# Self-attention over 4 x 4096 positions in float32: the weights' and x's split forms moved in SBUF to other addresses modulo 256 bytes

## The chip, the cores and the metric

One core of one Trainium2 chip. The metric is the device time of one execution in microseconds, as the median of several runs. Profiles are of one further execution, recorded by the hardware profiler.

## The reference

x has the shape (4, 64, 64, 256) in float32: B = 4 images of N = 4096 positions with C = 256 channels; q and k have C2 = 128 channels.

```python
q = jnp.einsum('bwhc,cd->bwhd', x, Wq) + bq
k = jnp.einsum('bwhc,cd->bwhd', x, Wk) + bk
v = jnp.einsum('bwhc,cd->bwhd', x, Wv) + bv
pq = q.reshape(B, -1, N)
pk = k.reshape(B, -1, N)
pv = v.reshape(B, -1, N)
energy = jnp.einsum('bcn,bcm->bnm', pq, pk)
attention = jax.nn.softmax(energy, axis=-1)
out = jnp.einsum('bcm,bnm->bcn', pv, attention)
out = out.reshape(B, W, H, C)
return gamma * out + x
```

## The kernel before

**Three forms of every operand.** Matmuls run on values of the type float32r. To keep float32's precision, each operand is split into three forms, numbered f = 0, 1, 2: h (the value scaled by a little under 1, rounded on writing), l (what is left) and d (a scaled difference of the two). A product of two operands is the sum of three matmuls, one for each f, added up in PSUM. The split is an ACT instruction (h) and two DVE instructions (l and d).

**Projections.** An image is projected in NI = 16 units i of 256 positions. For each unit, `transposed` (L186) makes four TensorE transposes into PSUM, `x_forms` (L193) splits the result into the tile `xf` of shape [128, 3, KC = 2, 2, 128], and `products` (L209) multiplies it with the weights' forms in the tile `wf` (L117). With w = 0 it makes q and k together: `xf` is the stationary operand, a 128x128 block, and the moving operand is `wf` of w = 0, 256 columns. With w = 1 it makes v: a 128x128 block of `wf` of w = 1 is stationary, and `xf` is moving, 256 columns. So each unit has 12 matmuls of 256 columns for each w, 24 in all, each with a weight load of its own, and the whole kernel has 1,536; they all stand at L222. The weights are split once, in `weights` (L159). DVE adds the bias of q and k in `seed_qk` (L233), ACT that of v in `seed_v` (L240), and `qk_forms` and `v_forms` split the results and send them to HBM (image 0 keeps v in SBUF).

**Attention.** The loop at L567 has B x STEPS = 512 steps n, 128 to an image: eight groups of 512 queries, and in each 16 steps over pairs of 128 keys. In a step, TensorE's work stands in this order: `cross` of step n+2 (L298, two matmuls, the part with f = 2 of the energies; ACT scales each at L299), `attend(n, 0)` (six matmuls at L355, accumulators `a` and `b`), `energy` of step n+2 (four matmuls at L313, f = 0 and 1; ACT's exponential at L316), what `step(n, "pe")` gives of the next image's projection, and `attend(n, 1)` (six more at L355). In `cross` and `energy` the stationary operand is the tile `k`, the moving one `q`; in `attend` the stationary operand is `vall` (named `v` in the profile) and the moving one `h` or `ld`, the forms of the exponentials, made by ACT (L322) and DVE (L336, L338). All these 9,216 matmuls have 512 columns. TensorE takes them in this order; a weight load for the next matmul can run while the present one streams.

**Projections between the steps.** Image 0 is projected ahead of the loop (L517 to L565). The units of image b+1 are spread over image b's steps, one unit to R = 8 steps: of the step's number r modulo 8, r = 0 transposes, r = 3 and 5 bring four products (f = 2) and r = 4 and 6 eight (f = 0 and 1). At the end of each group of 16 steps, `sums` (L384) adds up the softmax's denominators with two matmuls that have the constant `ones` as stationary operand and `zf` as moving one.

**Where the tiles lie.** A pool's tiles lie one behind the other in SBUF in the order in which their tags are first used, and the pools one behind the other: the constants, then `qkv` (`v`, `wf`), `ppool` (`x`, `ld`, `s`, `h`; the `xf` of image 0 uses `ld`'s buffers), `work` (`o`, `pf`, `q`, `xin`, `xf` of the other images, `r` with `zf`) and `kpool` (`k`). The constants end at byte 19,200 of each partition, 75 x 256. `ident` and `ones` start 128 bytes past a multiple of 256. Every tile of the later pools has a size that is a multiple of 256 bytes, so all of them start at a multiple of 256, and so does every slice that a matmul of L222, L298, L313 or L355 reads (the slices are steps of 512 or 1,024 bytes).

Of the kernel before, what the change touches and what calls it, by code (L numbers as in the profile page):

```python
# [10 lines left out]
F32R = mybir.dt.float32r  # L11
# [9 lines left out]
def kernel(  # L21
# [37 lines left out]
    B, W, H, C = x.shape  # L59
    P = 128  # L60
# [3 lines left out]
    KC = C // P  # L64
# [36 lines left out]
    with ExitStack() as fast:  # L101
# [4 lines left out]
        qkv = pool("qkv", 1)  # L106
        ppool = pool("ppool", 2)
        work = pool("work", 2)
# [5 lines left out]


        vall = qkv.tile([P, NU, 3, 2, C], F32R, tag="v", name="v")
        wf = qkv.tile([P, 2, 3, KC, C], F32R, tag="wf", name="wf")  # L117
        zd, rd = (dram.tile([B * NG, NB], F32, tag=n, name=n, bufs=1) for n in ("zd", "rd"))
        xs4 = work.tile([P, 4, 2, XB], F32, tag="o", name="xs", bufs=1)
        raw = ppool.tile([P, 2, KC, C], F32, tag="x", name="raw")  # L120
        scaled = ppool.tile([P, 2, KC, C], F32, tag="x", name="scaled")
# [29 lines left out]
        def split(h, l, d, y, scale=E):  # L151

            nc.scalar.activation(h, y, AF.Identity, scale=UPPER * scale)
            yield
            for t, f in ((d, 1.0 / scale + 1.0), (l, 1.0 / scale)):
                nc.vector.scalar_tensor_tensor(t, h.bitcast(F32), -f, y, ALU.mult, ALU.add)  # L156
                yield

        def weights(w):  # L159

            nc.scalar.mul(scaled[:, w], raw[:, w], E ** -(w + 1))
            yield from split(*(wf[:, w, f] for f in range(3)), scaled[:, w])

        def image(b):
            for g in range(NG):
# [5 lines left out]
        def bank(name, shape):  # L171
            pool, tag = next(now["banks"])
            return pool.tile(shape, F32, tag=tag, name=name)
# [19 lines left out]
        def x_forms(b, i):  # L193

            y = units.pop(("xt", b, i))
            if b == 0:
                f = ppool.tile([P, 3, KC, 2, P], F32R, tag="ld", name=f"xf_{b}_{i}")
            else:
                f = work.tile([P, 3, KC, 2, P], F32R, tag="xf", name=f"xf_{b}_{i}", bufs=1)
            units["xf", b, i] = f  # L200
            h = f[:, 0]
            nc.scalar.activation(h, y, AF.Identity, scale=UPPER)  # L202
            yield
            nc.vector.scalar_tensor_tensor(f[:, 2], h.bitcast(F32), 1.0 + E, y, ALU.mult, ALU.subtract)
            yield
            nc.vector.tensor_tensor(f[:, 1], y, h.bitcast(F32), ALU.subtract)
            yield

        def products(b, i, w, fs):  # L209

            xf = units["xf", b, i]
            if fs[0] == 2:
                units[w, b, i] = bank(f"qv{w}_{b}_{i}", [P, 2, C])
            to = units[w, b, i]
            for f in fs:
                for s in range(2):
                    for k in range(KC):
                        if w:
                            left, right = wf[:, 1, f, k, s * P : (s + 1) * P], xf[:, f, k]
                        else:  # L220
                            left, right = xf[:, f, k, s, :], wf[:, 0, f, k]
                        nc.tensor.matmul(  # L222
                            to[:, s, :],
                            left,
                            right.rearrange("p s a -> p (s a)") if w else right,
                            start=(f == 2 and s == k == 0),
                            stop=(f == 1 and k == KC - 1),
                            skip_group_check=True,
                        )
# [237 lines left out]
        def step(n, engine):  # L467
# [5 lines left out]
            if engine == "pe" and b < B:  # L473
                if r == 0:
                    transposed(b, i)
                elif r == 3:
                    products(b, i, 0, (2,))
                elif r == 4:
                    products(b, i, 0, (0, 1))
                elif r == 5:  # L480
                    products(b, i, 1, (2,))
                elif r == 6:
                    products(b, i, 1, (0, 1))
            elif engine == "act" and b < B:
                if r == 1:
                    made["x"] = x_forms(b, i)
                    next(made["x"])
                    load_x(b, i + 1)
                elif r == 5:
                    made["qk"] = qk_forms(b, i)  # L490
                    next(made["qk"])
                elif r == 6:
                    seed_v(b, i)
                elif r == 7:
                    made["v"] = v_forms(b, i)
                    next(made["v"])
            elif engine == "dve":
                if r == 0 and "v" in made:
                    for _ in made.pop("v"):
                        pass  # L500
                if b < B:
                    if r in (1, 2):
                        next(made["x"])
                    elif r == 3:
                        seed_qk(b, i)
                    elif r == 5:
                        next(made["qk"])
                    elif r == 6:
                        for _ in made.pop("qk"):
                            pass  # L510
                    elif r == 7:
                        next(made["v"])
# [6 lines left out]
        for i in range(3):  # L519
            load_x(0, i)  # L520
        transposed(0, 0)
        first = [weights(0), x_forms(0, 0), weights(1)]
        for pieces in first + [first[0], first[1], first[2]]:
            next(pieces)
        for pieces in first:
            next(pieces)
        for i in range(NI):
            load_x(0, i + 3)
            if i + 1 < NI:
                transposed(0, i + 1)  # L530
                xs = x_forms(0, i + 1)
            else:
                xs = iter(())
# [33 lines left out]
        for n in range(B * STEPS):  # L567
            b, u = divmod(n, STEPS)
# [42 lines left out]
    with tc.If(nc.values_load(again[0:1, 0:1]) > 0), ExitStack() as general:  # L611
# [3 lines left out]
        xpool, xtpool, qkv = pool("gx", 2), pool("gxt", 2), pool("gqkv", 1)  # L615
        ppool, work = pool("gp", NP + 2), pool("gw", 1)
# [86 lines left out]
        for b in range(B):  # L703
# [16 lines left out]
            for g in range(NG):  # L720
                ps = []
                mx = work.tile([P, 2, NB], F32, tag="mx", name=f"gmx_{b}_{g}")
                for t in range(NP):
# [9 lines left out]
                    p = ppool.tile([P, 2, NB], F32, tag="p", name=f"gp_{b}_{g}_{t}")  # L733
# [89 lines left out]
```

## Time and profile before

| | us |
|---|---|
| median of three runs | 2421.97 (2421.10 to 2422.91) |
| the profiled execution, its own time | 2424.35 |
| its span, first to last instruction | 2422.6 |

| lines | engine and operation | count | busy us | mean ns of one |
|---|---|---|---|---|
| L355 | PE matmul, 128x512, three groups | 6,144 | 640.0 + 633.4 + 631.7 | 390 to 394 |
| L313 | PE matmul, 128x512 | 2,048 | 552.0 | 391 |
| L298 | PE matmul, 128x512 | 1,024 | 316.3 | 390 |
| L222, w = 1 | PE matmul, 128x256 | 768 | 117.6 | 290 |
| L222, w = 0 | PE matmul, 128x256 | 768 | 113.9 | 285 |
| L222 | PE weight load, 128x128, both w | 1,536 | 109.1 + 108.8 | 194, 193 |
| L355 | PE weight load, 128x128, three groups | 6,144 | 385.1 + 383.9 + 369.3 | 188, 188, 189 |

Matmuls overlap in the pipeline, so the mean length of one (390 ns) is not the time between two: what counts for the whole is the distance from the start of one to the start of the next, called the pitch below. The granted TensorE clock has a mean of 0.994 of full speed over the span; it is at half speed for three short stretches in the first 114 us and for two at the end. The projection of image 0 fills the first 100 us, in which TensorE is busy for 66.89 us; between us 500 and 1000 it is busy for 495.48.

### The profile page before, as it was taken

To read this page: it belongs to the slowest core of one execution; us is meant where nothing else is said; L and a number is where in the kernel's file an instruction comes from. 1 tells how busy PE (TensorE), PEld (TensorE's weight loads), DVE (VectorE), ACT (ScalarE), POOL (GpSimd) and SP (SyncE) were. 2 spreads that over 40 slices of the span, in tenths; PEclk is the share of its full clock that TensorE was granted. 3 is DMA by queue.
4 is the path that set the end of the run, shared out by engine and by line. 5 is a ranking of instruction groups with operands and counts; after the bars stand their busy time and mean duration, and the time that the engine had idled before them with its cause. 6 is when DMAs were issued, how large, how long until landed. Compare 5 with 4: busy or idle time off the path is not lost.

```text
span 2422.6 us, 31905 instructions
## 1 busy us (share of the span) xinstructions
PE 2358.6 (97%) x11094; PEld 1954.4 (81%) x11094; DVE 2138.0 (88%) x2126; ACT 1870.8 (77%) x3076; POOL 581.7 (24%) x943
## 2 busy tenths in 40 slices
PE   6799999999999999999999999999999999999998
PEld 6688888888888888888888888888888888888886
DVE  7789988889989899888899898898888888888887
ACT  4577777877877877778778778778777778787875
POOL 5422222222322222212233122222123111111110
PEclk9999999999999999999999999999999999999999
DMA  9756655656796666566699566675569644444443
GB/s 200 169 143 166 180 143 158 177 156 181 217 296 171 168 164 181 146 158 178 157 284 265 147 165 166 170 181 147 154 176 315 198 127 131 120 119 125 120 123 92
DMA packets 243990, 413.82 MB, mean 171 GB/s; under 512 B 26031, under 2 KB 141487, under 8 KB 243822
## 3 DMA queue, kind: packets, MB, share of 16 engines
q0 software_dynamic: 203152, 368.77, 57.2%
q1 hardware_dynamic: 40126, 42.67, 6.4%
q8 instruction: 91, 1.49, 0.3%
q14 instruction: 77, 0.63, 0.1%
q10 hardware_dynamic: 544, 0.26, 0.0%
HBM read 306.64 MB, written 104.98 MB: 170 GB/s over the span
## 4 chain that ended last, share of the span: by engine, by line
PE 86%; ACT 9%; DMA 2%; DVE 1%; issue 1%; POOL 0%; SPq 0%; DVEq 0%; ACTq 0%
PE a L355 35%; PE b L355 17%; PE e L313 17%; PE e L298 9%; PE qv L222 7%; ACT o L369 3%; ACT e L299 2%; ACT x L316 1%; ACT h L322 1%; PE z L384 1%; PE xt L191 1%; DMA k<-kf 1%; DMA qd<-f 1%; ACT zf L378 1%; DVE v L156 0%
## 5 line engine op out<-in xcount | busy, mean ns | idle before, releaser
L316 ACT ACTIVATE x<-e 128x512 f32<-128x512 f32 x960 | 523.8, 600 | 319.1 <-PE e L313 316.0
L285 POOL DMA_DIRECT2D k<-kf x512 | 275.8, 539 | 1743.3 <-PE e L313 1638.6
L331 DVE TENSOR_TENSOR s<-s,x 128x1024 f32<-128x1024 f32 x480 | 585.8, 1220 | 95.1 <-ACT x L316 92.7
L299 ACT ACTIVATE e<-e 128x512 f32<-128x512 f32 x1024 | 547.4, 574 | 137.2 <-PE e L298 136.5
L355 PE MATMUL a<-h,v 128*128 128x512 f32 x2048 | 640.0, 394 | 0.0
L355 PE MATMUL a<-ld,v 128*128 128x512 f32 x2048 | 633.4, 390 | 0.0
L355 PE MATMUL b<-ld,v 128*128 128x512 f32 x2048 | 631.7, 390 | 0.0
L336 DVE TENSOR_TENSOR ld<-x,h 128x1024 fp32r<-128x1024 f32 x480 | 585.4, 1220 | 30.9 <-PE b L355 24.8
L338 DVE SCALAR_TENSOR_TENSOR ld<-h,x 128x1024 fp32r<-128x1024 f32 x480 | 584.4, 1218 | 0.0
L313 PE MATMUL e<-q,k 128*128 128x512 f32 x2048 | 552.0, 391 | 4.5
L322 ACT ACTIVATE h<-x 128x1024 fp32r<-128x1024 f32 x480 | 509.9, 1062 | 13.3
L313 PEld LDWEIGHTS e<-q,k 128*128 128x128 f32 x2048 | 379.4, 188 | 98.1 <-ACT e L299 23.2
L355 PEld LDWEIGHTS a<-ld,v 128*128 128x128 f32 x2048 | 385.1, 188 | 83.2
L355 PEld LDWEIGHTS b<-ld,v 128*128 128x128 f32 x2048 | 383.9, 188 | 82.8 <-ACT s L385 1.4
L355 PEld LDWEIGHTS a<-h,v 128*128 128x128 f32 x2048 | 369.3, 189 | 62.7 <-issue 1.0
L298 PE MATMUL e<-q,k 128*128 128x512 f32 x1024 | 316.3, 390 | 0.6 <-DMA k<-kf 0.6
L298 PEld LDWEIGHTS e<-q,k 128*128 128x128 f32 x1024 | 192.0, 188 | 42.3 <-issue 1.6
L222 PE MATMUL qv<-wf,xf 128*128 128x256 f32 x768 | 117.6, 290 | 26.0 <-DVE qv L233 25.9
L222 PEld LDWEIGHTS qv<-wf,xf 128*128 128x128 f32 x768 | 109.1, 194 | 37.4 <-DVE qv L233 29.5
L222 PEld LDWEIGHTS qv<-xf,wf 128*128 128x128 f32 x768 | 108.8, 193 | 7.5
L222 PE MATMUL qv<-xf,wf 128*128 128x256 f32 x768 | 113.9, 285 | 0.0
L270 POOL DMA_DIRECT2D kf<-f x128 | 98.4, 769 | 41.0 <-ACT xf L202 20.6
(79 smaller groups left out, 1215.1 us busy)
## 6 DMA issues: line engine op xcount, KB each, us to landing
k<-kf POOLq DMA_DIRECT2D x512, 384.0 KB, 3.5
vf<-vf POOLq DMA_DIRECT2D x48, 768.0 KB, 6.0
v<-vf POOLq DMA_DIRECT2D x48, 768.0 KB, 7.2
kf<-f POOLq DMA_DIRECT2D x128, 192.0 KB, 3.4
qd<-f POOLq DMA_DIRECT2D x128, 192.0 KB, 3.1
q<-qd POOLq DMA_DIRECT2D x32, 768.0 KB, 4.7
o<-in_x_dram POOLq DMA_DIRECT2D x31, 512.0 KB, 7.7
out_dram<-o SPq DMA_DIRECT2D x31, 512.0 KB
```

Of the source, the lines that this page charges most:

```text
L222: nc.tensor.matmul(to[:, s, :], left, right.rearrange("p s a -> p (s a)") if w else right, start=(f == 2 and s == k == 0), stop=(f == 1 an ...
L270: nc.gpsimd.dma_start(to, f)
L285: nc.gpsimd.dma_start(t, kf[b, u % NU])
L298: nc.tensor.matmul(e, *forms(n, i, 2), start=True, stop=False, skip_group_check=True)
L299: nc.scalar.mul(e, e, -REST)
L313: nc.tensor.matmul(e, *forms(n, i, f), start=False, stop=(f == 1), skip_group_check=True)
L316: nc.scalar.activation(x[:, i, :], e, AF.Exp, scale=(1.0 + E) ** 3 / E)
L322: nc.scalar.activation(h, units[n], AF.Identity, scale=UPPER)
L331: nc.vector.tensor_tensor(s, s, x, ALU.add)
L336: nc.vector.tensor_tensor(l, x, h.bitcast(F32), ALU.subtract)
L338: nc.vector.scalar_tensor_tensor(d, h.bitcast(F32), 1.0 + E, x, ALU.mult, ALU.subtract)
L355: nc.tensor.matmul(to, vall[:, t, f, i, j * P : (j + 1) * P], units[n][f][:, i, :], start=(t == 0 and i == 0 and f != 1), stop=(t == NU - ...
```

## The change

The tile `wf` becomes one flat row of 6 x KC x C + 32 elements (32 elements are 128 bytes). The forms of w = 1 (v) start at its beginning, those of w = 0 (q and k) behind them and 32 elements further. The tile `xf` becomes a flat row of XF = 6C + 16 elements (16 are 64 bytes), of which the forms take the last 6C. The instructions, their order and their shapes stay.

```diff
-        wf = qkv.tile([P, 2, 3, KC, C], F32R, tag="wf", name="wf")
+        wfs = qkv.tile([P, 6 * KC * C + 32], F32R, tag="wf", name="wf")
+        wf = [
+            wfs[:, o : o + 3 * KC * C].rearrange("p (f k c) -> p f k c", f=3, k=KC)
+            for o in (3 * KC * C + 32, 0)
+        ]
...
-            yield from split(*(wf[:, w, f] for f in range(3)), scaled[:, w])
+            yield from split(*(wf[w][:, f] for f in range(3)), scaled[:, w])
+
+        XF = 6 * C + 16
...
             if b == 0:
-                f = ppool.tile([P, 3, KC, 2, P], F32R, tag="ld", name=f"xf_{b}_{i}")
+                f = ppool.tile([P, XF], F32R, tag="ld", name=f"xf_{b}_{i}")
             else:
-                f = work.tile([P, 3, KC, 2, P], F32R, tag="xf", name=f"xf_{b}_{i}", bufs=1)
+                f = work.tile([P, XF], F32R, tag="xf", name=f"xf_{b}_{i}", bufs=1)
+            f = f[:, 16 : 16 + 6 * C].rearrange("p (f k s a) -> p f k s a", f=3, k=KC, s=2)
...
-                            left, right = wf[:, 1, f, k, s * P : (s + 1) * P], xf[:, f, k]
+                            left, right = wf[1][:, f, k, s * P : (s + 1) * P], xf[:, f, k]
                         else:
-                            left, right = xf[:, f, k, s, :], wf[:, 0, f, k]
+                            left, right = xf[:, f, k, s, :], wf[0][:, f, k]
```

## The prediction

> **What bounds the kernel.** I read the page's busy shares first, then the chain that ended last by engine, then that chain in order of time around the lines that the change touches, then the nanosecond start times of the matmuls there.
>
> ```profile
> PE 2358.6 (97%) x11094; PEld 1954.4 (81%) x11094; DVE 2138.0 (88%) x2126; ACT 1870.8 (77%) x3076; POOL 581.7 (24%) x943
> ...
> PE 86%; ACT 9%; DMA 2%; DVE 1%; issue 1%; POOL 0%; SPq 0%; DVEq 0%; ACTq 0%
> ```
>
> TensorE is the bound: 97% busy and 86% of the chain. The time is therefore the number of matmuls times the distance from one start to the next (below: the pitch). No matmul is added or removed, so only the pitch can change. The chain in order of time shows it (start us, length us, what):
>
> ```profile
> 1111.67 0.91 PE a L355 x4
> 1112.58 0.45 PE b L355 x2
> 1113.03 0.91 PE e L313 x4
> 1113.94 0.47 PE qv L222 x4
> 1114.41 0.93 PE a L355 x4
> 1115.34 0.46 PE b L355 x2
> 1115.80 0.45 PE e L298 x2
> 1116.25 0.91 PE a L355 x4
> 1117.16 0.45 PE b L355 x2
> 1117.61 0.91 PE e L313 x4
> 1118.52 0.95 PE qv L222 x8
> ```
>
> Two things are to be seen. Eight 256-wide products of L222 take 0.95, 119 ns each, while four 512-wide matmuls take 0.91, 227 ns each, or 113.5 per 256 columns: the products cost more per column. And right behind products the four `a` matmuls take 0.93 and the two `b` 0.46, against 0.91 and 0.45 elsewhere.
>
> In nanoseconds, as medians over the 48 groups of each kind behind us 100: the undisturbed pitch of a 512-wide matmul is 226.7. A group of four products has 113.4, 119.1, 120.0, 120.0; a group of eight goes on at 120.0. The next five 512-wide matmuls have 233.3, 235.9, 228.4, 232.5, 230.9, and the sixth is back at 226.7. These are the same in all groups to 1 ns, for both kinds of product (w=0 and w=1).
>
> 113.4 is half of 226.7 although each of both runs beside one weight load of the same size, so I take 113.4 per 256 columns as the floor of the moving stream. In the half-clock slices at the start the pitch is 213 and 427, one column per 0.833 ns, without any surplus: what stretches the pitch at full clock is the supply of operands, not the array. What lies above the floor (6.7 per product, up to 9.2 behind them) differs with the moment at which the weight load meets the running stream. The change can act here if that meeting depends on addresses.
>
> **What moves.** From the tile sizes, every tile ahead of and between the pools is a multiple of 256 bytes before, so every operand of L222, L298, L313 and L355 starts at residue 0 modulo 256. Afterwards `wf` is 128 bytes longer, so all that lies behind it moves: `x`, `ld`, `s`, `h`, `q`, `xin` to 128; the `xf` tile is 64 bytes longer and its data lie 64 in, at 192 for image 0 (in an `ld` buffer) and for the others; `r`, `zf` and `k` to 192. `v` and the v form of `wf` stay at 0, the q and k form goes to 128. Stationary minus moving residue then is: products w=1, 0-192 = 64; products w=0, 192-128 = 64; L298 and L313 (`k` against `q`), 64; L355 (`v` against `h` or `ld`), 128. So not 1,536 matmuls change their alignment but all 10,752.
>
> **The cost, part by part.**
> 1. Products behind us 100: 1,152, in 96 groups of four and 96 of eight. Surplus over 113.4 of a group of four 0+5.7+6.6+6.6 = 19 ns, of eight 19+4×6.6 = 45 ns: 96×64 = 6.2 us. If the two streams no longer meet, all of it goes: -6.2 us.
> 2. The five matmuls behind each group: 6.6+9.2+1.7+5.8+4.2 = 27.5 ns, 192 groups: 5.3 us. Four products at 113.4 take exactly two pitches of 226.7 and eight take four, so if step 1 holds the order in which both streams were before is kept, and these go too: -5.3 us.
> 3. Products before us 100: surplus 1.9 us by the same start times. PE waits there for L233 (the table of waits: us in total, times, longest), so a shorter product mostly lengthens that wait; taken as 0, at best -1.9.
>
> ```profile
> PE qv L222 <- DVE qv L233: 25.9, 15, 4.5
> ```
>
> 4. Attention, 9,216 matmuls (L298 1,024, L313 2,048, L355 6,144): undisturbed at the floor now, so there is nothing to win, but each ns lost costs 9.2 us. The nearest row for another residue is L384: `ones` is at 128 and `zf` at 0 (the timeline: start us, length us, instructions, idle time before).
>
> ```profile
> 178.01 0.30 PEld L384 LDWEIGHTS z<-zf,ones 128*128 128x128 f32 x2 [0.89 <-ACT o L369]
> 178.01 0.73 PE L384 MATMUL z<-zf,ones 128*128 128x512 f32 x2 [0.45 <-ACT o L369]
> 178.35 0.59 PEld L191 LDWEIGHTS xt<-ident,x 128*128 128x128 f32 x4
> ```
>
> From the second weight load to the second matmul the 31 pairs have 228 to 236 ns. The first matmul of L313 or L355 behind a pause, at residue 0, has 227 to 240 by the same measure. So 128 apart shows neither better nor worse than 0, at the one moment it can be seen. I take 0 for attention. The bounds: the worst pitch in any row is 235.9, +9.2×9,216 = +85 us; the other way, down to the 213.3 of one column per cycle, -13.3×9,216 = -123 us, which the equal cost per column at 256 and 512 wide speaks against.
> 5. Transfers into moved tiles (`k`, `q`, `xin`, `o`): nothing, since PE waited 0.6 us in all for `k`, which lands in 3.5 us with a step of 4.5 us and three buffers ahead. Without that cover a doubled landing would cost at most 3.5 us per late `k`. DVE and ACT keep their instructions; at 88% and 77% they follow a PE that gains 0.5%.
>
> Sum: -6.2-5.3 = -11.5 us. The profiled execution has 2424.35 us with a span of 2422.6, so 2412.9 and 2411.1; against the median of 2421.97, **2410.5 us**.
>
> The Trainium skill speaks against any effect: "TensorE: Matmul & The Clock Gate", step-by-step list of Part 2, says that TensorE reads moving and stationary operand through two independent SBUF ports and that loading the next weights takes no bandwidth from the running matmul. By that rule the sum would be 0. The surplus of 6.6 ns behind the second product is not explained by it, and no row here shows whether addresses are the cause.
>
> **The rivals.**
> - *The residue changes nothing.* The surplus could come from widths alone: a 256-wide pitch leaves 113 ns for a weight load of about 106 (from the load to the first matmul behind a pause), so each product's stream has a load beside it nearly all the time. For it: w=0 and w=1 have the same pitch though operands swap sides. Against: the first product of each group also carries a full load and sits at the floor. Then products and the five behind them stay: 2422, or 2419 to 2425 with a shifted order. The skill's two ports give the same time.
> - *Attention loses its order (slower).* All operands share one residue now, and every run between disturbances settles to exactly 226.7. After the change, the pair of moving and stationary residue switches from 128 to 64 and back four times per step (from `b` to L298, back to `a`, from `b` to L313, back to `a`). If a switch disturbs the order as a group of products does, its first two matmuls cost 6.6+9.2 = 15.8 ns: 512 steps × 4 × 15.8 = +32 us; less the 11.5 won, **2443 us**. If no stretch of two to six matmuls ever settles, the mean of the five, 5.5 ns, holds for all 9,216: +51 us, 2473. It decides from 1.25 ns per attention matmul (11.5/9,216); from 1.8 ns the kernel is slower by over 0.2%. For it: five to nine matmuls pass after every pause until the pitch is back at 226.7. Against: L384's row above.
> - *Attention gains as well:* 2350 or so, half of the bound in step 4; nothing but the missing row for residue 64 speaks for it.
>
> **Chances.** Forecast (products to the floor, attention as before) 0.45; attention loses its order 0.41; no effect 0.10; attention gains 0.04. What a measurement of this kernel can tell from no change is about 0.2%, 4.8 us. Faster: 0.45 less 0.02 for a partial gain under that bound, plus 0.04 = 0.47; same 0.10+0.02 and less 0.01 for the shifted order = 0.11; slower 0.42. The forecast's own range is 2406 to 2417: from all surplus gone with the 1.9 us of step 3 and some 3 us of the same surplus behind pauses, to half of the gain. The range for 8 in 10 reaches into the slower case, past its 2443, to 2462, which leaves out its upper quarter and the gain on attention: 2405 to 2462.
>
> **What would show it.** Step 1: eight products in the chain at 0.91 instead of 0.95. Step 2: `a` behind products at 0.91, not 0.93. Step 4: four `a` elsewhere still 0.91 and four L313 0.91; if these read 0.93 or more, attention lost its order and the forecast is wrong on the slower side. If everything reads as before, the residue does not matter. PE's waits for `k` above a few us would make step 5 wrong.

## The result and the profile after

| | before | changed |
|---|---|---|
| median, us | 2421.53 (2419.73 to 2422.91, 4 runs) | 2463.19 (2462.48 to 2464.26, 4 runs) |
| span of the profiled execution, us | 2422.6 | 2460.7 |

The changed kernel is slower by the ratio 1.0174, with a 95% interval of 1.0161 to 1.0186. Its line numbers differ, as do those of the kernels further down: L222 has become L229, L298 L305, L313 L320 and L355 L362.

The page's busy shares, its chain by engine and three of its groups, of the changed kernel:

```profile
PE 2399.0 (97%) x11094; PEld 1952.7 (79%) x11094; DVE 2142.7 (87%) x2126; ACT 1875.3 (76%) x3076; POOL 582.7 (24%) x943
...
PE 87%; ACT 9%; DMA 1%; DVE 1%; issue 1%; POOL 0%; SPq 0%; DVEq 0%; ACTq 0%
...
L362 PE MATMUL a<-ld,v 128*128 128x512 f32 x2048 | 647.2, 397 | 0.0
...
L320 PE MATMUL e<-q,k 128*128 128x512 f32 x2048 | 563.8, 397 | 1.5 <-ACT e L306 0.3
...
L362 PEld LDWEIGHTS a<-ld,v 128*128 128x128 f32 x2048 | 386.9, 189 | 89.8
```

TensorE is the bound as before, with the same number of instructions and 40 us more of busy time (2399.0 against 2358.6); DVE and ACT differ by 5 us. The matmuls of `ld` with `v` take 397 ns where they took 390, those of `q` with `k` 397 where they took 391. The weight load beside them has stayed at 188 to 189 ns.

The chain in order of time, the changed kernel around its products:

```profile
1127.79 0.46 PE b L362 x2
1128.25 0.93 PE e L320 x4
1129.18 0.47 PE qv L229 x4
1129.66 0.92 PE a L362 x4
1130.58 0.46 PE b L362 x2
1131.04 0.46 PE e L305 x2
1131.50 0.94 PE a L362 x4
1132.44 0.46 PE b L362 x2
1132.90 0.93 PE e L320 x4
1133.83 0.94 PE qv L229 x8
```

The four `a` of 1131.50, with eight matmuls between them and the last product, take 0.94 where the kernel before had 0.91 in that place, four L320 take 0.93 where L313 had 0.91, two L305 0.46 where L298 had 0.45. The eight products take 0.94 instead of 0.95. So it is not the products, for whose operands the pads were put in, that changed most, but attention's matmuls.

A stretch without any product shows it alone: the last image's steps have none. The windows of both kernels, first before, then changed (us, busy time and number of PE, PEld, DVE, ACT and POOL, granted clock, DMA share, GB/s):

```profile
1900.00:2400.00 500.00, 495.84 (x2170) 404.79 (x2169) 436.70 (x390) 394.25 (x641) 74.75 (x132) 1.00 0.48 126
```

```profile
1900.00:2400.00 500.00, 496.07 (x2115) 395.57 (x2114) 426.82 (x383) 388.77 (x629) 78.62 (x139) 1.00 0.50 131
```

In the same 500 us, at the same granted clock of 1.00, TensorE starts 2,115 matmuls instead of 2,170, though it is as busy.

Nearly all of the time can be booked from the start times of the matmuls. The sums of the pitches behind us 100 (a matmul in front of a pause is counted at 226.7 ns and the rest as the pause):

| us | before | changed | difference |
|---|---|---|---|
| `v` with `h` and `ld` (6,144 matmuls, L355 and L362) | 1399.8 | 1429.3 | +29.5 |
| `k` with `q` (3,072, less those before us 100) | 695.1 | 711.8 | +16.7 |
| products, of v (w=1) and of q and k (w=0) | 69.0 + 68.4 | 66.9 + 68.1 | -2.4 |
| pauses | 41.0 | 35.3 | -5.7 |
| transposes, sums of the denominators | 37.5 | 37.0 | -0.5 |

Together +37.6; the last matmul starts 37.5 us later, and the spans differ by 38.1. (The medians differ by 41.7, as the profiled execution before was longer than its median.) In steps without products or pauses (some 250 in each profile) a matmul of attention took 226.9 ns on average before and 232.7 after, and there is no longer any position in the step with a median at 226.7.

### The profile page after: what moved, and what is told of

Read it like the earlier page. It is cut to its first block, busy times and chain, and to the rows that moved or that the text cites. A ratio compares the mean times of both kernels' runs of the same rounds, so it can differ in the third digit from the quotient of the medians.

```text
span 2460.7 us, 31905 instructions
## 1 busy us (share of the span) xinstructions
PE 2399.0 (97%) x11094; PEld 1952.7 (79%) x11094; DVE 2142.7 (87%) x2126; ACT 1875.3 (76%) x3076; POOL 582.7 (24%) x943
## 4 chain that ended last, share of the span: by engine, by line
PE 87%; ACT 9%; DMA 1%; DVE 1%; issue 1%; POOL 0%; SPq 0%; DVEq 0%; ACTq 0%
PE a L362 36%; PE b L362 18%; PE e L320 17%; PE e L305 9%; PE qv L229 6%; ACT o L376 3%; ACT e L306 2%; ACT x L323 1%; ACT h L329 1%; DMA qd<-f 1%; PE z L391 1%; PE xt L197 1%; ACT zf L385 1%; ACT vf L157 0%; DVE qv L240 0%
## 5 line engine op out<-in xcount | busy, mean ns | idle before, releaser
L362 PE MATMUL a<-ld,v 128*128 128x512 f32 x2048 | 647.2, 397 | 0.0
L362 PE MATMUL a<-h,v 128*128 128x512 f32 x2048 | 645.5, 396 | 0.0
L362 PE MATMUL b<-ld,v 128*128 128x512 f32 x2048 | 641.0, 394 | 0.0
L320 PE MATMUL e<-q,k 128*128 128x512 f32 x2048 | 563.8, 397 | 1.5 <-ACT e L306 0.3
L320 PEld LDWEIGHTS e<-q,k 128*128 128x128 f32 x2048 | 379.6, 188 | 106.9 <-ACT e L306 21.4
L362 PEld LDWEIGHTS b<-ld,v 128*128 128x128 f32 x2048 | 384.4, 188 | 94.4 <-ACT s L392 1.4
L362 PEld LDWEIGHTS a<-ld,v 128*128 128x128 f32 x2048 | 386.9, 189 | 89.8
L362 PEld LDWEIGHTS a<-h,v 128*128 128x128 f32 x2048 | 367.5, 188 | 69.3 <-issue 0.5
L305 PE MATMUL e<-q,k 128*128 128x512 f32 x1024 | 320.4, 394 | 0.0
L305 PEld LDWEIGHTS e<-q,k 128*128 128x128 f32 x1024 | 191.8, 188 | 45.3 <-issue 0.6
L229 PE MATMUL qv<-wf,xf 128*128 128x256 f32 x768 | 117.2, 290 | 27.3 <-DVE qv L240 27.2
L229 PEld LDWEIGHTS qv<-wf,xf 128*128 128x128 f32 x768 | 109.0, 194 | 39.8 <-DVE qv L240 30.6
L229 PEld LDWEIGHTS qv<-xf,wf 128*128 128x128 f32 x768 | 107.2, 191 | 8.3
L229 PE MATMUL qv<-xf,wf 128*128 128x256 f32 x768 | 110.9, 280 | 0.0
L386 DVE TENSOR_TENSOR zf<-s,zf 128x512 fp32r<-128x512 f32 x31 | 21.5, 693 | 99.6 <-ACT zf L385 99.6
```

Source lines behind the costliest of these rows:

```text
L229: nc.tensor.matmul(to[:, s, :], left, right.rearrange("p s a -> p (s a)") if w else right, start=(f == 2 and s == k == 0), stop=(f == 1 an ...
L305: nc.tensor.matmul(e, *forms(n, i, 2), start=True, stop=False, skip_group_check=True)
L320: nc.tensor.matmul(e, *forms(n, i, f), start=False, stop=(f == 1), skip_group_check=True)
L362: nc.tensor.matmul(to, vall[:, t, f, i, j * P : (j + 1) * P], units[n][f][:, i, :], start=(t == 0 and i == 0 and f != 1), stop=(t == NU - ...
```

## The experiments

"Difference" below is the start of the stationary operand minus that of the moving one, modulo 256 bytes. All kernels are the one before with other places for its tiles, and leave nothing out. The times are medians of four executions or more, of two for the differences 32 and 224 below. A ratio is against the kernel before, measured beside.

**Only the products' operands.** The form of the weights for q and k goes ahead of the constants, where it lies at 128; x's forms lie at 192; `kpool` is placed ahead of `work`, so that `k` stays at 0.

```diff
+    wf0 = const.tile([P, 3, KC, C], F32R, name="wf0")
     ident = const.tile([P, P], F32, name="ident")
...
-        wf = qkv.tile([P, 2, 3, KC, C], F32R, tag="wf", name="wf")
+        wf = [wf0, qkv.tile([P, 3, KC, C], F32R, tag="wf", name="wf")]
...
-                f = work.tile([P, 3, KC, 2, P], F32R, tag="xf", name=f"xf_{b}_{i}", bufs=1)
+                f = work.tile([P, 6 * C + 48], F32R, tag="xf", name=f"xf_{b}_{i}", bufs=1)
+            f = f[:, 48 : 48 + 6 * C].rearrange("p (f k s a) -> p f k s a", f=3, k=KC, s=2)
```

> Only the products' operands get the change's residues (q and k weights' form 128, v's 0, x's forms 192, so stationary minus moving 64 in both); v, h, ld, q and k stay at 0. Theory A (the loss is attention's, whose moving and stationary operands no longer share one residue modulo 256): attention's pitch back at 226.7 to 227.6 ns and the time at 2416 to 2424 us. Rival B (the products at another residue disturb the stream that follows them): at least 20 us of the 41 us lost remain, 2440 us or more.

Measured: 2419.60 us against 2420.78, ratio 0.9995 (0.9986 to 1.0005). The mean pitch of all attention matmuls, but for those in front of a pause, is 227.7 ns, against 227.6 in the kernel before and 232.7 in the changed one. The chain in order of time of this kernel:

```profile
1111.19 0.91 PE e L315 x4
1112.10 0.47 PE qv L224 x4
1112.58 0.93 PE a L357 x4
1113.50 0.46 PE b L357 x2
1113.97 0.45 PE e L300 x2
1114.42 0.91 PE a L357 x4
...
1115.78 0.91 PE e L315 x4
1116.69 0.94 PE qv L224 x8
```

The undisturbed `a` and `e` are back at 0.91; behind products `a` still reads 0.93. Theory A holds, B falls: the loss is attention's. Also, the move as intended is worth nothing that can be measured: the surplus over the floor within the products fell from 6.2 to 5.3 us, and in the eight matmuls behind them it rose from 5.3 to 6.4.

**Only attention's operands.** The pad of 128 bytes stands ahead of both weights' forms, the 64 bytes of the `xf` tile behind the forms, so the products' operands all lie at 128 and attention's where the change put them.

```diff
+        wfs = qkv.tile([P, 6 * KC * C + 32], F32R, tag="wf", name="wf")
+        wf = [
+            wfs[:, o : o + 3 * KC * C].rearrange("p (f k c) -> p f k c", f=3, k=KC)
+            for o in (32, 32 + 3 * KC * C)
+        ]
...
+            f = f[:, 0 : 0 + 6 * C].rearrange("p (f k s a) -> p f k s a", f=3, k=KC, s=2)
```

> Only attention gets the change's residues (h, ld, q 128, k 192, v 0); the weights' and x's forms share one residue, 128. Theory A: attention's mean pitch 232 to 233 ns as in the changed kernel, and 2463 to 2468 us, since the products lose what little they had won. Rival B: attention near 227.6 ns and the time within 10 us of 2421.5.

Measured: 2465.47 us, ratio 1.0184 (1.0167 to 1.0201), attention at 232.6 ns by the same mean. As theory A expected: this is the whole loss.

**One pair at a time.** First all tiles behind `v` at 128 (the last kernel's `wf`, with the old `xf`): difference 128 for L355's matmuls, 0 for those of `q` and `k`.

> All tiles behind v at 128, v at 0: the pair of L355 differs by 128, that of q and k by 0, and the step has four switches between the two. Theory A1 (each switch disturbs the order): surplus on both kinds of matmul, those of q and k too, 30 to 50 us slower than before. Theory A2 (a pair is slow because it differs, wherever it stands): only L355's matmuls above 226.7, those of q and k within 1 ns of it; 6144 x 6 ns = 37 us slower if 128 is a bad difference, and 0 if 64 was the bad one.

Then `k` at 64 (the old `wf`, 64 bytes behind the forms in the `xf` tile; of the other tiles only that of `r` and `zf` moves with it): difference 64 for `q` and `k`, 0 for L355's.

> Only k moved, to 64, with q, v, h and ld at 0: the pair of q and k differs by 64, that of L355 by 0. Theory A1 (switches): surplus on both kinds, 30 to 50 us slower. Theory A2 (the pair's own difference): only L298 and L313 above 226.7, 3072 x 6 ns = 18 us slower if 64 is a bad difference, and 0 if not.

Measured: 2455.61 us, ratio 1.0144 (1.0127 to 1.0161), and 2454.94 us, ratio 1.0141 (1.0124 to 1.0158). Both kinds of matmul lose in both kernels, and both times lie where A1 put them, 35 and 34 us above the kernel before; A2, which left out the other pair, had the time right for the first (37) and not for the second (18). With `v` against the rest, its matmuls rose by 28.2 us (1399.8 to 1428.0), and those of `q` and `k`, whose difference is 0, by 7.3 (695.1 to 702.4). With `k` against the rest, its own rose by 16.3 (to 711.4), and L355's, with difference 0, by 19.2 (to 1419.0). That is 4.6 and 5.3 ns for a matmul with a difference, and 2.4 and 3.1 for one without. In the second kernel an access of ACT or DVE can hardly be the cause: they touch neither `k` nor `q`, and the tile of `r` and `zf` only once in 16 steps. The first kernel's chain:

```profile
1110.15 0.46 PE e L302 x2
1110.62 0.93 PE a L359 x4
1111.55 0.46 PE b L359 x2
1112.01 0.91 PE e L317 x4
```

Here four matmuls of `q` and `k` read 0.91. In nanoseconds they go 231, 227, 227 and then 232 at the next switch: with difference 0 they are back at the floor after one or two, and each stretch of six with difference 128 pushes them off again. So a pair that differs spoils its neighbours. That it would be slow without any switch these two kernels do not show.

**One difference for all pairs.** If only the switches cost, a kernel with a single difference other than 0 must be as fast as before. `kpool` goes ahead of `ppool`, with a gap of 192, 128 or 64 bytes between them: `v` and `k` at 0, `h`, `ld`, `q` and x's forms at 192, 128 or 64. For 64 and 192 the weights' form of q and k lies at 128, as in the first experiment, so the products have the same difference.

```diff
+        kpool = pool("kpool", 3)
+        gap = pool("gap", 1)
+        gap.tile([P, 48], F32, tag="gap", name="gap")
         ppool = pool("ppool", 2)
         work = pool("work", 2)
-        kpool = pool("kpool", 3)
```

> Stationary minus moving is 64 for every pair of the kernel: v, k and v's weights' form at 0, h, ld, q and x's forms at 192, q and k weights' form at 128. Theory A1 (only the switches of the difference within the stream cost): attention settles at 226.7 to 227.6 ns, products near 113 to 118, 2405 to 2422 us. Theory A2 (a difference of 64 costs in itself): attention above 230 ns, 2450 us or more.

> Stationary minus moving is 128 for every pair: v, k and the weights' forms at 0, h, ld, q and x's forms at 128. Theory A1: as with 64, 2405 to 2422 us. Theory A2: attention above 230 ns, 2450 us or more.

> Stationary minus moving is 192 for every pair: v, k and v's weights' form at 0, q and k weights' form at 128, h, ld, q and x's forms at 64. Theory A1: 2405 to 2422 us. Theory A2: slower for 64 and 128 and this one; if this one alone is at 2421 or below, the sign of the difference matters.

And all operands 128 bytes further, which leaves every difference at 0:

```diff
-        vall = qkv.tile([P, NU, 3, 2, C], F32R, tag="v", name="v")
+        vs = qkv.tile([P, NU * 6 * C + 32], F32R, tag="v", name="v")
+        vall = vs[:, 32:].rearrange("p (t f i c) -> p t f i c", t=NU, f=3, i=2)
```

> All operands 128 bytes further, so that every difference stays 0 (but for the constant that sums the denominators, whose difference goes from 128 to 0). Theory A, both forms: as before, 2419 to 2424 us, with products at 113, 119, 120 and attention at 227. Rival C (the residue of the address itself costs, whatever the other operand's is): 2440 us or more.

Then the same gap with 224 and 32 bytes, to see 32 bytes to either side of 0 (the means that the next text names are over all attention matmuls, those of the table below over the steps without products or pauses):

> Stationary minus moving is 32 for every pair of attention: v and k at 0, h, ld and q at 224 (products: 32 for v's, 224 for those of q and k). With 0, 64, 128 and 192 measured at mean pitches of 227.6, 233.3, 232.8 and 229.3 ns, a theory in which the cost follows the difference in steps of 64 bytes (whole lines) expects 32 to cost as 64, 2460 to 2470 us; one in which it grows smoothly from 0 expects 229 to 231 ns, 2435 to 2455 us; one in which only equal residues are free expects anything above 2435 us.

> Stationary minus moving is 224 for every pair of attention: v and k at 0, h, ld and q at 32. Steps of 64 bytes: as 192, 2430 to 2440 us, or as 0, 2418 to 2423 us. Smooth: 228 ns, 2424 to 2430 us. A pitch below 226.6 ns would show that 226.7 is no floor.

| difference of attention's pairs | us | ratio (95%) | mean pitch in plain steps, ns |
|---|---|---|---|
| 0, all at 0 (before) | 2420.55 | | 226.9 |
| 0, all at 128 | 2422.53 | 1.0007 (0.9997 to 1.0016) | 226.7 |
| 32 | 2469.34 | 1.0202 (1.0181 to 1.0222) | 233.3 |
| 64 | 2468.08 | 1.0196 (1.0179 to 1.0214) | 233.3 |
| 128 | 2466.71 | 1.0189 (1.0172 to 1.0206) | 232.9 |
| 192 | 2434.72 | 1.0057 (1.0041 to 1.0074) | 228.9 |
| 224 | 2470.44 | 1.0206 (1.0186 to 1.0226) | 233.3 |

The ratios of 32 and 224 are against 2421.14 us, those of the others against 2420.55. The chain of the kernel with 64 for all, of that with 192 for all, and of that with all operands at 128:

```profile
1115.48 0.93 PE a L358 x4
1116.41 0.47 PE b L358 x2
1116.88 0.93 PE e L316 x4
```

```profile
1115.37 0.91 PE a L358 x4
1116.28 0.46 PE b L358 x2
1116.74 0.91 PE e L316 x4
```

```profile
1116.53 0.91 PE a L356 x4
1117.43 0.45 PE b L356 x2
1117.88 0.91 PE e L314 x4
```

Theory A1 falls: with 64 for all pairs nothing switches, and all matmuls are slow. They are even settled: in a step the pitches alternate between 231 and 235 (medians). At 192 they repeat 229, 229, 230, too little above 226.7 to be seen in the chain's hundredths. So a difference costs by itself, and A2 is left; a switch costs the neighbours besides. Rival C falls too: with all operands at 128 the time is the same within the interval, so what counts is the one operand's address against the other's. Of the theories of the size two miss: 32 costs as much as 64, but 224 costs more than 192, so neither whole lines of 64 bytes nor a smooth growth from 0 describes it. That only equal residues are free agrees with all five differences. No difference has a mean below 226.7.

The modulus itself is not shown. In the kernel before all tiles behind the constants have sizes that are multiples of 512 bytes, and their slices are steps of 512 or 1,024. So wherever the difference of attention or the products is called 0, the two starts lie a multiple of 512 apart, and in no kernel do they lie 256 apart. With a period of 512 the rows 32, 64, 128, 192 and 224 of the table would be called 288, 320, 384, 448 and 480, and the 64 of `k` alone would stay 64, another distance than that of the table.

**Attention at 0, the products at other differences.** First, both kinds of product at 192 (as the first experiment, with x's forms at 64 instead of 192); then x's forms alone moved by 64, with both weights' forms at 0.

> Attention at difference 0, the products at 192 (v's weights' form 0, x's forms 64, those of q and k 128). From the kernel in which all pairs had 192: v's products 118 ns, those of q and k 113 to 114 in groups of eight. Theory: each boundary between attention and products switches the difference, so the five or so matmuls behind keep their surplus, and the gain stays under 5 us: 2416 to 2422 us. If the order survives the switch: 2411 to 2415 us.

> Only x's forms move, by 64 bytes, with attention and both weights' forms at 0: v's products have stationary minus moving 192, those of q and k 64. If the small gain of the version with all products at 192 (0.9988 of before) comes from the products' own difference, v's products read 118.0 ns and those of q and k 117.7, and the ratio is 0.998 to 1.000. If it came from the surplus behind the products, which was smaller at 192 for all, only half of it is kept: 0.999 to 1.000. Above 1.001 neither holds.

Measured: 2417.66 us, ratio 0.9988 (0.9978 to 0.9997), and 2417.92 us, ratio 0.9991 (0.9982 to 1.0000). Products are at 118.0 (q and k) and 118.3 ns (v) in both, against 118.75 before; the products of 113 to 114 ns that the first expectation names were v's, by the tiles that the trace names, and they did not come back. The ratio of the second lies in both of its expected ranges, and the pitches say that both parts contribute. The surplus within the products is 5.5 us in both, behind them 3.5 and 4.5 us, against 6.2 and 5.3 before: some 2.5 and 1.5 us, of the 11.5 that lay over the floor. The first is the only version whose whole interval lies below the kernel before, by some 3 us, at the edge of what can be measured.

## Why the prediction was wrong, point by point

**What bounds the kernel** was right: TensorE's pitch is the time, and the whole difference is found in it. That alignment counts for 10,752 matmuls and not for 1,536 was right as well, and decided the result.

**Step 1** (products to the floor, -6.2 us) had the direction and not the size: -2.4 us in the changed kernel, and with the products' operands alone moved the surplus within them fell by 0.9. The products of v do reach 113 ns in the changed kernel, but only from the fourth of a group on (122, 116, 114, 113); those of q and k stay at 117 to 121. Both differ by 64 modulo 256, but by 320 and 64 modulo 512; with the products alone moved both differ by 320, and both stay at 117 and more, so what decides between 113 and 117 stays open. (The profile names the moving operand first, as its first products show, which the program makes with w = 0: `qv<-wf,xf`, busy for 117.6 us in the table of the time before, is w = 0, and `qv<-xf,wf`, 113.9 us, is w = 1; the table has the two the other way round.)

**Step 2** (the five matmuls behind, -5.3 us) failed with it: with the products alone moved, the surplus in the eight matmuls behind a group is 6.4 us in all instead of 5.3.

**Step 4** is the step that failed. Attention was taken at 0, "nothing to win", and lost 46.2 us (29.5 and 16.7), 5.0 ns for each of its matmuls. It was taken at 0 because of L384, the one row with a difference of 128. That row was read right behind a pause, where difference 0 reads 227 to 240 ns as well: both are unsettled there, so the row could not tell one from the other. What mattered, the pitch at which a long run settles, was seen for difference 0 only. The upper bound of +85 us had its place; the value between the bounds should not have been 0, since every attention matmul was leaving the only difference at which the floor had been seen. The other bound, -123 us, was rightly not believed: no mean pitch lies below 226.7 at any of six differences.

**Step 3 and step 5** held: from the first to the last product of image 0's projection it is 89.0 us before and 89.5 in the changed kernel, where 0 was taken; and TensorE has no wait for `k` in the changed kernel's table of waits, while that of the products for the bias on DVE is 27.2 us, after 25.9 before.

**The rivals.** The slower one named the place, attention, and its two prices, 2443 and 2473, lie to either side of the measured 2463.19. (The 2473 leaves out the 11.5 us won that the 2443 counts; with them it is 2461.) Its mechanism was half of it. Switches of the difference do disturb pairs whose own difference is 0 (+7.3 and +19.2 us in the two experiments with one pair moved), but a stream without switches is as slow. That its 5.5 ns for each matmul came near the measured 5.0 is luck: it was the mean of five matmuls behind products, all with difference 0. The range for 8 in 10 ended at 2462, inside this case, and was left by 1.2 us. That the residue changes nothing is refuted by every kernel in which attention's pairs differ. By the rule of the Trainium skill that was set against the change ("TensorE: Matmul & The Clock Gate", step-by-step list of Part 2: two independent ports, and loading the next weights takes no bandwidth from the running matmul) the sum was 0. The trace disagrees with that sum: with the same instructions, and weight loads of 188 ns throughout, the mean pitch of a 512-wide matmul goes from 226.7 to 233.3 ns with the address of the weights against that of the stream.

That the two reads get in each other's way is what these numbers suggest; no run here took the weight load away from beside a matmul, so whether and how they meet stays open, and also why 192 costs a third of what the other differences cost. The prediction's reading that the supply of operands stretches the pitch at full clock is in the same state: it fits, and no run shows it.

## What to carry to other kernels

A pad in one tile moves every tile behind it: list the start of every operand of the bounding engine modulo a few hundred bytes before and after, and price the largest group first. In this kernel the two operands of an attention matmul should start a multiple of 512 bytes apart, the only distance at which their floor was measured; two per cent of the time hang on it, and twenty times less on the operands that the pad was put in for. A row read at a disturbed moment says nothing about a settled stream. Where the settled value is not in the trace, the term is unknown: with 9,216 instructions behind it, it belongs into the sum by its bounds and not as 0.

## What the hardware did that was not expected

The pitch of float32r matmuls of 512 columns, each with a weight load of its own, depends on the difference of the two operands' start addresses: 226.7 to 226.9 ns at a multiple of 512 bytes and, counted modulo 256, 228.9 at 192, 232.9 at 128 and 233.3 at 32, 64 and 224, as means over steps without products or pauses. A move of all operands by 128 bytes together left it at 226.7 ns. In the kernel before, a stream with difference 0 took five matmuls behind products and mostly six to ten behind a pause to settle at its pitch.
